# Layer 0 attention: later exponentials and totals in the short rows, and the quotient written over its own PSUM bank

## The chip, the cores and the metric

One core of one Trainium2 chip. The metric is the device time of one execution in microseconds (us). Times inside the execution come from one profiled run; "ns" is used for single instructions. The engines are called PE (matmul), PEld (its weight load), DVE (vector), ACT (scalar), POOL (GpSimd) and SP (it issues the DMAs).

## The reference, cut to what matters

Two layers are added to an input x of shape 1 x 128 x 256 x 256. The change touches layer 0 alone:

```
# layer 0; x is group-normalised first; 128 rows s, 256 positions r, 8 heads of 32 channels
bias   = einsum('nijz,zh->nhij', pair_repr, bias_proj)
gate   = sigmoid(msa @ gate_proj)
q,k,v  = split(msa @ qkv_proj)
sim    = softmax(einsum('nsqhc,nskhc->nshqk', q, k) / sqrt(32)) + bias
attend = einsum('nshqk,nskhc->nsqhc', sim, v) * gate
x      = x + attend @ out_proj
```

The softmax is not divided before the product with v. With E the exponentials of the scores, a row is computed as (E v) / (sum of E) + (bias v), then gated. Layer 1 is a banded attention of 4 heads with 64 channels; its code is not changed.

## The kernel before, in words

**Rows and pairs.** The loop at line 1092 runs over the 128 rows s. Projections are made for two rows at once, in a form with seven products instead of eight (class `Seven`, lines 592 to 634). A pair of rows has one *even* row, in whose second half the projections q and k of a later pair are made ("qk", order EARLY), and one *odd* row with v and the gate ("vg", order PLAIN) and the output projection of an older pair. The even row is the short one.

**Order within a row s.** On PE: scores of heads 0 to 3 (`sim`, line 837), row sums of the row before (`zs`, line 882), in odd rows one product of bias and values (`pbv`, line 933), E v of the row before (`av`, line 869), scores of heads 4 to 7, then the *stretch*, a list of projection products of about 0.43 us each (line 590) with bias products among them. PE, ACT, DVE and SP follow the program's order exactly, since the block at line 1078 is scheduled by hand; POOL is not in that list.

**The stretch.** `two_of_them` (line 639) reads the order string word by word. `fA` and `gA` are the first two products of the two projections f and g, followed by an ACT copy of the whole bank (line 622). `f3`, `f6`, `f7`, `f4`, `f2` are single products; after 6 and 7 ACT copies half a bank to `mid` (lines 624, 626), after 4 a whole bank (line 628). `x` calls `rest`, `d` takes the next job from `work`, `b` the next bias product, `p` the next output product. The products accumulate in one bank, so product 3 overwrites half of the bank only after the copy at 622, product 7 only after the copy at 624, and product 4 only after the copy at 626.

**ACT's exponentials.** Each half of a row has four banks of scores; one exponential (line 850) empties one. Three are issued at once, the fourth in the first half of a row after `join_tiles`, in the second half at `x`. `totals` (line 983) follows at `x`: ACT copies the sums `zs` of the row before and also writes out the accumulated sum, which the profile shows as a second instruction at line 988.

**DVE's chain.** `divide` (line 958) takes the reciprocal of `zs` and sends it through DRAM so that it comes back spread over all partitions as `near`. `weighted` (line 1005) multiplies `av` by `near` (line 1011). `gated` runs two rows later, as the first of a row's own DVE work: it adds bias times values (line 1022) and multiplies by the gate (line 1023). `least` (line 991) takes the smallest sum.

**PSUM.** Eight banks: five in a ring shared by scores and projections, and one each for `z`, `bv` and `av`. With one bank for `av`, the `av` product of a row starts when every reader of the older one has finished; before, the last reader is the product in `weighted`, which writes to a tile `t` in SBUF.

The lines that set this up in a row are:

```python
last_exp = scores(s, 0)
gated(s - 2)
zs = sum_heads(s - 1)
divide(s - 1, zs)
...
attend(s - 1)
```

Of the kernel before, what the change touches and what calls it, by code (L numbers as in the profile page):

```python
# [9 lines left out]
F32 = mybir.dt.float32  # L10
AF = mybir.ActivationFunctionType
ALU = mybir.AluOpType
# [3 lines left out]
P = 128  # L16
R = 256
# [22 lines left out]
def conv_preact_kernel(  # L40
# [14 lines left out]
    nc = tc.nc  # L55
    S = x.shape[1]
# [69 lines left out]
    for part, first in ((seen[:, 0], 0), (seen_high, -KB)):  # L126
        nc.gpsimd.memset(part, 1.0)
        for b in range(NB):
            d = first + KB * b - QLO[b]
# [504 lines left out]
            nc.gpsimd.tensor_tensor(self.to[:, 2:4], self.to[:, 2:4], self.mid, ALU.add)  # L634

    PLAIN = "fA gA x f2 p f3 f6 p g3 g6 p f7 b p g7 f4 p b g4 p g2 b p"
    EARLY = "fA gA x d b f3 f6 g3 g6 d f7 f2 g7 f4 b d g4 g2 d b"

    def two_of_them(pool, f, g, name, order, rest, bias, po, work):

# [133 lines left out]
    with ExitStack() as both:  # L774
# [21 lines left out]
        with ExitStack() as lay0:  # L796
            row = lay0.enter_context(tc.tile_pool(name="row0", bufs=2))
            att = lay0.enter_context(tc.tile_pool(name="att0", bufs=2))
            st, hd, outs = {}, {}, {}
# [29 lines left out]
            def scores(s, half):  # L829
                i, r = divmod(s, 2)  # L830
                q, k = res["q", i], res["k", i]
                sims = [sim_bank(f"sim{s}_{half}_{j}") for j in range(4)]
                for kt in range(2):
                    for c in range(2):
                        for j in range(4):
                            p0, k0 = D0 * j, kt * P + KB * c
                            nc.tensor.matmul(  # L837
                                sims[j][KB * c : KB * (c + 1), kt, :],
                                lhsT=k[p0 : p0 + D0, 2 * r + half, k0 : k0 + KB],
                                rhs=q[p0 : p0 + D0, 2 * r + half, :],  # L840
                                start=True, stop=True,
                            )
                ex = att.tile([P, 4, 2, R], F32, tag="ex", name=f"ex{s}_{half}", bufs=3)
                both = att.tile([P, 4, R], F32, tag="both", name=f"both{s}_{half}")
                hd[s, half] = (ex, both)


                def weigh(js):
                    for j in js:
                        nc.scalar.activation(ex[:, j], sims[j], AF.Exp, scale=1.0 / math.sqrt(D0))  # L850

                weigh(range(3))
                return lambda: weigh((3,))

            def join_tiles(s, half, j):

                if s < S:
                    ex, both = hd[s, half]
                    nc.vector.tensor_tensor(both[:, j : j + 2], ex[:, j : j + 2, 0, :], ex[:, j : j + 2, 1, :], ALU.add)  # L859
# [98 lines left out]
            def divide(s, zs):  # L958
                if s < 0:
                    return  # L960
                rz = att.tile([P, R], F32, tag="rz", name=f"rz{s}", bufs=1)
                nc.vector.reciprocal(rz, zs[:, 0, :])  # L962
                near = att.tile([P, 2, R], F32, tag="near", name=f"near{s}", bufs=1)
                if s < S - 1:
                    far = rz0_far[s % 2]
                    nc.sync.dma_start(out=far.rearrange("j h q -> (j h) q"), in_=rz[0 : P : B // 2])
                    for j in range(A):
                        nc.sync.dma_start(
                            out=near[strip(j)].rearrange("p h q -> p (h q)"),
                            in_=far[j].rearrange("h q -> (h q)").partition_broadcast(B),  # L970
                        )
                hd[s, "rz"] = rz
                hd[s, "z"] = (zs, near)

            def spread_last(s):

                rz, near = hd[s, "rz"], hd[s, "z"][1]
                ps = proj_bank(f"near{s}")
                for half in range(2):
                    nc.tensor.matmul(ps[:, half, :], lhsT=spread0[:, half], rhs=rz, start=True, stop=True)  # L980
                nc.scalar.copy(near, ps)

            def totals(s):

                if s >= 0:
                    zs = hd[s, "z"][0]
                    z = att.tile([P, R], F32, tag="z", name=f"z{s}", bufs=1)
                    nc.scalar.activation(z, zs[:, 0, :], AF.Identity, accum_out=zsum[:, s : s + 1])
                    hd[s, "least"] = z

            def least(s):

                if s >= 0:
                    z = hd.pop((s, "least"))
                    nc.vector.tensor_reduce(zmin[:, s : s + 1], z, axis=AX.X, op=ALU.min)
# [9 lines left out]
            def weighted(s):  # L1005

                if s < 0:
                    return
                av, near = hd.pop((s, "av")), hd.pop((s, "z"))[1]
                t = hd[s, "t"] = att.tile([P, 2, R], F32, tag="t", name=f"t{s}", bufs=1)  # L1010
                nc.vector.tensor_tensor(t, av, near, ALU.mult)  # L1011

            def gated(s):

                if s < 0:
                    return
                i, r = divmod(s, 2)
                if r == 0:
                    ats[i] = row.tile([P, 4, R], F32, tag="at", name=f"at{i}", bufs=1)
                st[s]["at"] = at = ats[i][:, 2 * r : 2 * r + 2, :]  # L1020
                t = hd.pop((s, "t"))
                nc.vector.tensor_tensor(t, hd.pop(s), t, ALU.add)  # L1022
                nc.vector.scalar_tensor_tensor(  # L1023
                    at, res["g", i][:, 2 * r : 2 * r + 2, :], 1.0, t, op0=ALU.add, op1=ALU.mult
                )
# [52 lines left out]
            with tc.manual_schedule(  # L1078
# [11 lines left out]
                nc.sync.dma_start(out=bias_far, in_=bias_blocks[0, 1])  # L1090
                most1 = Most(st1, stats1, 3, 1)
                for s in range(S):
                    last_exp = scores(s, 0)
                    gated(s - 2)
                    zs = sum_heads(s - 1)
                    divide(s - 1, zs)
                    join_tiles(s, 0, 0)
                    last_exp()
                    if s % 2 == 1:
                        e = res["g", s // 2]  # L1100
                        nc.scalar.activation(e, e, AF.Tanh, scale=0.5)
                    if s % 2 == 0:
                        bias = biased(s // 2)
                    else:
                        next(bias)
                    attend(s - 1)
                    join_tiles(s, 0, 2)
                    if s == 0:
                        sum_bias()
                    if s % 2 == 0:  # L1110
                        settle_pair((s - 4) // 2)
                    if S - 3 <= s < S - 1:
                        most1.join(s - S + 3)
                    normal(s + 4)
                    last_exp = scores(s, 1)
                    if s == 4:
                        for weights in quarters1.values():
                            weights.sum()
                    work = (
                        lambda: join_tiles(s, 1, 0), lambda: join_tiles(s, 1, 2),  # L1120
                        lambda: weighted(s - 1), lambda: least(s - 1),
                    )

                    def rest():

                        last_exp()
                        totals(s - 1)

                    po = iter(())
                    if s % 2 == 1 and s > 1:  # L1130
                        out_sums((s - 3) // 2)
                        po, work = output((s - 3) // 2, work), ()
                    if s < S - 2:
                        stretch(
                            ("qk", "vg")[s % 2], s // 2 + 1, (EARLY, PLAIN)[s % 2], rest, bias, po,
                            work if s % 2 == 0 else (),
                        )
                        work = work if s % 2 == 1 else ()
                    else:
                        rest()  # L1140
                        for _ in range(2 if s % 2 == 0 else 3):
                            next(bias)
                            next(po, None)
                            next(po, None)
                        for _ in po:
                            pass
                        if s % 2 == 0:
                            next(bias)
                    for job in work:
                        job()  # L1150
                    if s % 2 == 1 and s < S - 2:
                        sum_rows((s + 3) // 2)
                        sum_values(s // 2 + 1)
# [7 lines left out]
                        nc.tensor.matmul(warm[:, 0, :], lhsT=ident, rhs=out_sb[:, 0, :], start=True, stop=True)  # L1161

                gated(S - 2)
                divide(S - 1, sum_heads(S - 1))
                totals(S - 1)
                attend(S - 1)
# [17 lines left out]
        with ExitStack() as lay:  # L1184
# [4 lines left out]
            att = lay.enter_context(tc.tile_pool(name="att1", bufs=2))  # L1189
# [268 lines left out]
            with tc.manual_schedule(engines={  # L1458
# [12 lines left out]
                for i in range(last):  # L1471
                    s = 2 * i
# [266 lines left out]
```

## Time and profile before

| what | value |
|---|---|
| median of 3 runs | 3120.62 us (3120.52 to 3124.83) |
| the profiled execution's own time | 3121.14 us |
| its span, first to last instruction | 3119.4 us |
| exponentials of layer 0 (line 850) | from 209.2 to 2028.0 us, 1024 of them |
| granted TensorE clock, mean | 0.992 |
| DVE, busy from 430 to 830 us | 353.85 us |
| ACT, busy from 430 to 830 us | 270.06 us |
| POOL, busy from 430 to 830 us | 272.73 us |
| L962 reciprocal, 128 of them | 1745 ns each |
| L995 smallest sum, mean | 408 ns each |

The profiled execution takes 1.7 us more than its span, which lies outside the first and the last instruction. In a timeline a line has the start in us from the span's start, the duration, the engine, the source line, the operation and the tiles (output, arrow, inputs); "idle before" is in square brackets. A matmul's end is modelled and overlaps the next one's start, so the spacing of starts tells how fast PE really goes. `x8` or `x16` are the instructions merged into the line.

### The profile page before, as it was taken

Reading aid. Unit: us, or ns where it says so; the run is one execution under the profiler, and the core shown is the slowest. Engines: PE = TensorE matmul, PEld = TensorE weight load, DVE = VectorE, ACT = ScalarE, POOL = GpSimd, SP = SyncE. Lnnn points to the kernel's source line nnn. Section 1 sums busy time; section 2 is a strip of 40 time slices with the busy share of each in tenths; the row PEclk is TensorE's granted clock in tenths of the full one; section 3 lists DMA queues with packets and bytes.
Section 4 is the critical chain, followed back from the end, with each engine's and each line's share of the span. In section 5 each row is a group of like instructions: output and inputs, shape, how many; then the busy total and the mean of one; then the engine's idle time right before and its main releaser. Section 6 shows DMA issues by size and latency. Waiting matters only on the chain.

```text
span 3119.4 us, 142735 instructions
## 1 busy us (share of the span) xinstructions
PE 3028.8 (97%) x62733; PEld 2048.6 (66%) x62733; DVE 2422.4 (78%) x4523; ACT 1904.3 (61%) x4321; POOL 2015.4 (65%) x1916
## 2 busy tenths in 40 slices
PE   6779999999999999999999999999999999999997
PEld 4546666666666666666666666567777777777775
DVE  4668888888888888898888888856666666666665
ACT  4656666666666666666666666645555555555553
POOL 3036667666766666676667666647677777777774
PEclk8989999999999999999999999999999999999999
DMA  9942222222222222222122222124444444444443
GB/s 375 424 129 55 50 65 61 57 55 65 61 50 62 65 61 49 63 65 61 48 65 62 60 51 65 41 65 98 104 99 103 99 96 104 100 101 100 96 102 71
DMA packets 384790, 280.86 MB, mean 90 GB/s; under 512 B 285232, under 2 KB 353312, under 8 KB 378016
## 3 DMA queue, kind: packets, MB, share of 16 engines
q1 hardware_dynamic: 383264, 269.29, 33.0%
q8 instruction: 494, 8.09, 1.1%
q0 software_dynamic: 752, 2.36, 0.2%
q14 instruction: 136, 1.11, 0.1%
q10 hardware_dynamic: 144, 0.00, 0.0%
HBM read 202.38 MB, written 69.18 MB: 87 GB/s over the span
## 4 chain that ended last, share of the span: by engine, by line
PE 91%; DMA 5%; DVE 2%; POOL 1%; issue 1%; ACT 0%; SPq 0%; DVEq 0%; POOLq 0%; ACTq 0%
PE sim L837 8%; PE p1v L1260 7%; PE av L869 7%; PE p1q L590 7%; PE pbv L933 6%; PE po L590 6%; PE pq L590 6%; PE p1o L590 6%; PE p1k L590 6%; PE pv L590 6%; PE pk L590 5%; PE pg L590 5%; PE zs L882 4%; PE 1sim L1281 3%; DMA pr<-in_L_conv_pair_repr_dram 3%; PE 1av L1322 3%
## 5 line engine op out<-in xcount | busy, mean ns | idle before, releaser
L850 ACT ACTIVATE ex<-sim 128x512 f32<-128x512 f32 x1024 | 549.8, 608 | 281.2 <-PE sim L837 281.2
L859 DVE TENSOR_TENSOR both<-ex 128x512 f32<-128x512 f32 x512 | 471.0, 948 | 13.4 <-ACT ex L850 13.2
L634 POOL TENSOR_TENSOR v<-v,midv 128x512 f32<-128x512 f32 x64 | 82.3, 1285 | 401.1 <-ACT v L628 401.1
L837 PE MATMUL sim<-q,k 32*64 32x256 f32 x8192 | 289.8, 389 | 1.3 <-ACT ex L850 1.3
L869 PE MATMUL av<-ex,v 128*32 128x256 f32 x4096 | 244.5, 379 | 0.0
L1291 POOL TENSOR_TENSOR 1p<-1ex,seen 128x768 f32<-128x768 f32 x127 | 231.5, 1823 | 12.5 <-ACT 1ex L1289 12.5
L694 ACT ACTIVATE 1q<-p1q,bqk 128x256 f32<-128x256 f32 x192 | 90.9, 473 | 240.2 <-PE p1q L590 121.8
L1260 PE MATMUL p1v<-w_in_t,1xn 128*64 128x128 f32 x4096 | 236.3, 273 | 0.1
L1260 PEld LDWEIGHTS p1v<-w_in_t,1xn 128*64 128x64 f32 x4096 | 231.5, 137 | 6.0 <-issue 0.5
L962 DVE RECIPROCAL rz<-zs 128x256 f32<-128x256 f32 x128 | 223.3, 1745 | 6.1 <-PE zs L882 6.1
L582 POOL TENSOR_TENSOR 1ts<-1xn 128x512 f32<-128x512 f32 x64 | 81.3, 1271 | 226.8 <-ACT 1xn L1221 226.8
L837 PEld LDWEIGHTS sim<-q,k 32*64 32x64 f32 x8192 | 152.4, 131 | 113.5 <-issue 41.9
L1023 DVE SCALAR_TENSOR_TENSOR at<-g,t 128x512 f32<-128x512 f32 x128 | 202.6, 1583 | 9.2 <-DVE t L1022 0.5
L1391 DVE TENSOR_TENSOR 1at<-1av,1near 128x512 f32<-128x512 f32 x128 | 82.5, 686 | 137.2 <-DMA 1near<-rz_far 108.3
L634 POOL TENSOR_TENSOR q<-q,midq 128x512 f32<-128x512 f32 x64 | 82.2, 1285 | 157.9 <-ACT q L628 157.9
L869 PEld LDWEIGHTS av<-ex,v 128*32 128x32 f32 x4096 | 131.8, 110 | 77.1 <-DVE t L1011 0.5
L1298 POOL TENSOR_TENSOR 1zp<-1p 128x512 f32<-128x512 f32 x127 | 162.4, 1278 | 10.0
L1267 ACT COPY 1v<-p1v 128x512 f32<-128x512 f32 x128 | 75.0, 586 | 125.0 <-PE p1v L1260 125.0
L346 DVE BATCH_NORM_STATS2 stats<-xs 128x6 f32<-128x128 f32 x512 | 100.3, 277 | 64.7 <-DMA xs<-in_x_dram 64.7
L723 DVE TENSOR_TENSOR o<-po,xt 128x256 f32<-128x256 f32 x189 | 80.2, 424 | 77.8 <-PE po L590 72.0
L882 PE MATMUL zs<-both,place 128*32 128x256 f32 x2048 | 138.8, 388 | 0.5 <-DVE both L859 0.5
L688 DVE SCALAR_TENSOR_TENSOR 1o<-p1o,bo_v,yg 128x256 f32<-128x256 f32 x183 | 88.5, 483 | 56.0 <-PE p1o L590 53.2
(340 smaller groups left out, 8564.4 us busy)
## 6 DMA issues: line engine op xcount, KB each, us to landing
pr<-in_L_conv_pair_repr_dram SPq DMA_DIRECT2D x32, 1024.0 KB
xs<-in_x_dram SPq DMA_DIRECT2D x16, 2048.0 KB
x<-o SPq DMA_DIRECT2D x64, 512.0 KB
yg<-x SPq DMA_DIRECT2D x64, 512.0 KB
out_dram<-1o SPq DMA_DIRECT2D x256, 128.0 KB
near<-rz_far SPq DMA_DIRECT2D x508, 64.0 KB
xg<-in_x_dram SPq DMA_DIRECT2D x252, 128.0 KB
1near<-rz_far SPq DMA_DIRECT2D x124, 256.0 KB
```

Source lines behind the costliest of these rows:

```text
L590: nc.tensor.matmul(out[cols], lhsT=lhsT[:, cols], rhs=rhs, **flags)
L634: nc.gpsimd.tensor_tensor(self.to[:, 2:4], self.to[:, 2:4], self.mid, ALU.add)
L837: nc.tensor.matmul(sims[j][KB * c : KB * (c + 1), kt, :], lhsT=k[p0 : p0 + D0, 2 * r + half, k0 : k0 + KB], rhs=q[p0 : p0 + D0, 2 * r + ha ...
L850: nc.scalar.activation(ex[:, j], sims[j], AF.Exp, scale=1.0 / math.sqrt(D0))
L859: nc.vector.tensor_tensor(both[:, j : j + 2], ex[:, j : j + 2, 0, :], ex[:, j : j + 2, 1, :], ALU.add)
L869: nc.tensor.matmul(to[D0 * j : D0 * (j + 1), half, :], lhsT=v[:, 2 * r + half, c0 : c0 + D0], rhs=weights(4 * half + j, kt), start=(kt == ...
L882: nc.tensor.matmul(zs[strip(j), 0, :], lhsT=place0[:, half, :], rhs=both[:, j, :], start=(half == 0), stop=(half == 1),)
L933: nc.tensor.matmul(ps[strip(j), acc, half, :], lhsT=stationary[n][:, half, strip(j)], rhs=bias_of[n][:, 4 * half + j, :], start=(n <= 2 an ...
L962: nc.vector.reciprocal(rz, zs[:, 0, :])
L1023: nc.vector.scalar_tensor_tensor(at, res["g", i][:, 2 * r : 2 * r + 2, :], 1.0, t, op0=ALU.add, op1=ALU.mult)
L1260: nc.tensor.matmul(ps[KB * half : KB * (half + 1), b, :], lhsT=xns[i][:, 2 * r + kt, KB * b : KB * (b + 1)], rhs=w_in_t[:, kt, 2 * C + P * ...
L1291: engine.tensor_tensor(p.rearrange("p j (r c) -> p (j r) c", c=WROW)[:, :, 0 : 2 * WSTEP] .rearrange("p r (t c) -> p r t c", c=WSTEP)[:, : ...
```

## The change

Five things are edited, all in layer 0.

1. The exponentials. `scores` now issues two at once and returns the other two. In the first half of a row both follow after `join_tiles`. In the second half of odd rows (and of the last two rows) the third is issued at once and the fourth at `x`, as before. In the second half of even rows the order string has two `x`: the third comes between the copy of `fA` and the copy of `gA`, the fourth after the copy of `g6`.
2. `totals` moves from `x` to the end of the stretch, after its last copies.
3. `least` leaves the list of jobs and runs one row later, after the second `join_tiles`; for row S - 2 it runs after the loop.
4. In EARLY the bias product after `gA` comes ahead of the first job, and the later jobs are moved by a few places. The order of the PE products is the same.
5. The quotient (product of `av` and `near`) is written over `av` in its PSUM bank, the addition of `gated` works in place there, and the tile `t` is gone.

```diff
-    EARLY = "fA gA x d b f3 f6 g3 g6 d f7 f2 g7 f4 b d g4 g2 d b"
+    EARLY = "fA x gA b d f3 f6 g3 g6 x f7 f2 g7 f4 d b g4 d g2 b"
...
-                weigh(range(3))
-                return lambda: weigh((3,))
+                weigh(range(2))
+                return (lambda: weigh((2,))), (lambda: weigh((3,)))
...
-                av, near = hd.pop((s, "av")), hd.pop((s, "z"))[1]
-                t = hd[s, "t"] = att.tile([P, 2, R], F32, tag="t", name=f"t{s}", bufs=1)
-                nc.vector.tensor_tensor(t, av, near, ALU.mult)
+                av, near = hd.pop((s, "av")), hd.pop((s, "near"))
+                nc.vector.tensor_tensor(av, av, near, ALU.mult)
+                hd[s, "t"] = av
...
-                nc.vector.tensor_tensor(t, hd.pop(s), t, ALU.add)
+                nc.vector.tensor_tensor(t, t, hd.pop(s), ALU.add)
...
-                    last_exp = scores(s, 0)
+                    exps = scores(s, 0)
                     gated(s - 2)
                     zs = sum_heads(s - 1)
                     divide(s - 1, zs)
                     join_tiles(s, 0, 0)
-                    last_exp()
+                    for exp in exps:
+                        exp()
...
                     attend(s - 1)
                     join_tiles(s, 0, 2)
+                    least(s - 2)
...
-                    last_exp = scores(s, 1)
+                    third, fourth = scores(s, 1)
+                    if s % 2 == 1 or s >= S - 2:
+                        third()
...
                     work = (
                         lambda: join_tiles(s, 1, 0), lambda: join_tiles(s, 1, 2),
-                        lambda: weighted(s - 1), lambda: least(s - 1),
+                        lambda: weighted(s - 1),
                     )
 
+                    rests = iter((third, fourth) if s % 2 == 0 and s < S - 2 else (fourth,))
+
                     def rest():
 
-                        last_exp()
-                        totals(s - 1)
+                        next(rests)()
...
+                    totals(s - 1)
                     for job in work:
                         job()
...
                 gated(S - 2)
+                least(S - 2)
                 divide(S - 1, sum_heads(S - 1))
                 totals(S - 1)
```

More of the change, by code (lines that the diff above doesn't have):

```diff
@@ L972, in divide @@
                 hd[s, "rz"] = rz
-                hd[s, "z"] = (zs, near)
+                hd[s, "zs"], hd[s, "near"] = zs, near
             def spread_last(s):
-                rz, near = hd[s, "rz"], hd[s, "z"][1]
+                rz, near = hd[s, "rz"], hd[s, "near"]
                 ps = proj_bank(f"near{s}")
@@ L985, in totals @@
                 if s >= 0:
-                    zs = hd[s, "z"][0]
+                    zs = hd.pop((s, "zs"))
                     z = att.tile([P, R], F32, tag="z", name=f"z{s}", bufs=1)
```

## The prediction, made before the changed kernel ran

> **What bounds the kernel now.** I read the page's busy times and its chain of work first, then busy time by window, then the timeline of one pair of rows engine by engine, and last the single lines of DVE.
>
> ```profile
> PE 3028.8 (97%) x62733; PEld 2048.6 (66%) x62733; DVE 2422.4 (78%) x4523; ACT 1904.3 (61%) x4321; POOL 2015.4 (65%) x1916
> PE 91%; DMA 5%; DVE 2%; POOL 1%; issue 1%; ACT 0%; SPq 0%; DVEq 0%; POOLq 0%; ACTq 0%
> ```
>
> PE carries the chain. In the middle of layer 0 the windows show it busy without a break, at full clock:
>
> ```profile
> 430.00:830.00 400.00, 400.00 (x9455) 253.95 (x9450) 353.85 (x534) 270.06 (x604) 272.73 (x254) 1.00 0.25 59
> ```
>
> That busy share hides small waits, since matmuls overlap. They show in the spacing of starts. An even row begins at 1011.52 and the next at 1040.00, so a pair takes 28.47 us, the same from pair to pair. A projection product takes 0.43 us from start to start; in the even row some starts come later:
>
> ```profile
> 1013.46 1.91 PE L869 MATMUL av<-ex,v 128*32 128x256 f32 x32
> 1018.10 0.62 PE L933 MATMUL pbv<-bias_sb,v 128*32 128x128 f32 x16
> 1018.64 0.64 PE L590 MATMUL pq<-xn,sums_q 128*32 128x256 f32 x8
> 1019.10 0.61 PE L590 MATMUL pq<-ts,sums_q 128*32 128x256 f32 x8
> ...
> 1019.96 0.61 PE L590 MATMUL pk<-ts,sums_k 128*32 128x256 f32 x8
> 1020.54 0.64 PE L590 MATMUL pq<-ts,sums_q 128*32 128x256 f32 x8
> 1021.00 0.61 PE L590 MATMUL p2qk<-xn,qkv_sb 128*32 128x256 f32 x8
> ```
>
> The step to 1018.64 (product f3) is 0.54 and the one after it 0.46; the step to 1020.54 (f7) is 0.58 and the next 0.46. Against 0.433 this is 0.107 + 0.027 + 0.147 + 0.027 = **0.31 us in each pair**. The list of waits names ACT for both, and ACT's timeline says why:
>
> ```profile
> PEld pq L590 <- ACT midq L624: 27.3, 63, 0.4
> PEld pq L590 <- ACT q L622: 11.9, 62, 0.2
> ```
>
> ```profile
> 1017.98 0.61 ACT L622 COPY q<-pq 128x512 f32<-128x512 f32 x1
> ...
> 1018.92 0.66 ACT L850 ACTIVATE ex<-sim 128x512 f32<-128x512 f32 x1
> 1019.41 0.45 ACT L988 ACTIVATE z<-zs 128x256 f32<-128x256 f32 x1
> 1019.68 0.26 ACT L988 ACTIVATION_READ_ACCUMULATOR z<-zs 128x1 f32 x1
> 1019.77 0.43 ACT L943 COPY bv<-pbv 128x256 f32<-128x256 f32 x1
> 1020.12 0.37 ACT L624 COPY midq<-pq 128x256 f32<-128x256 f32 x1
> 1020.70 0.37 ACT L624 COPY midk<-pk 128x256 f32<-128x256 f32 x1 [0.21 <-PE pk L590]
> ```
>
> The copy of fA ends at 1018.59 behind three exponentials, and f3 starts 0.05 later. The copy after f6 ends at 1020.49 behind the fourth exponential and the totals, and f7 starts 0.05 later. The odd row shows no such step. DVE is late nowhere for PE, but slow in the gate's two instructions:
>
> ```profile
> 1011.66 0.42 DVE L723 TENSOR_TENSOR o<-po,xt 128x256 f32<-128x256 f32 x1 [0.88 <-PE po L590]
> 1012.00 1.17 DVE L1022 TENSOR_TENSOR t<-bv,t 128x512 f32<-128x512 f32 x1
> 1013.28 1.58 DVE L1023 SCALAR_TENSOR_TENSOR at<-g,t 128x512 f32<-128x512 f32 x1
> ```
>
> ```profile
> L1011 DVE TENSOR_TENSOR t<-av,near x128: 676/680/692, 243.6 to 2040.2; 128x512 f32<-128x512 f32 x128
> L1022 DVE TENSOR_TENSOR t<-bv,t x128: 679/792/1522, 244.6 to 2040.9; 128x512 f32<-128x512 f32 x128
> L1023 DVE SCALAR_TENSOR_TENSOR at<-g,t x128: 691/1592/1658, 246.2 to 2041.6; 128x512 f32<-128x512 f32 x128
> ```
>
> [...] L1022 and L1023, both inputs in SBUF, spread from 0.68 to 1.5 and 1.66 us; L1011, with `av` in PSUM, never leaves 676 to 692 ns, also at 1023.39, where POOL's sum over q is running. [...]
>
> **The change, part by part.**
>
> *Gain, f3 and f7.* The exponentials of this half start at 1016.54 and follow each other by 0.49, so with two of them ahead the copy of fA starts at 1017.52 (its second product ends at 1016.80 + 0.61) and ends at 1018.13, ahead of f3's due time 1018.10 + 0.43. The totals leave, so the copy after f6 follows f6 freely and f7 doesn't wait. That removes 0.31.
>
> *New wait, f4.* The fourth exponential now stands between the copy after g6 and the copy after f7, and f4 overwrites what the latter reads. From the start of g6: the copy starts 0.74 later (1019.96 to 1020.70); a 256-column instruction gives way after 0.27 (1019.41 to 1019.68), so the exponential starts at 1.01; the next starts 0.49 after it (1018.92 to 1019.41), at 1.50; the copy after f7 takes 0.37 and PE 0.05 more, 1.92. f4 is due four products after g6, at 1.73. That is 0.19, and 0.027 for the longer step behind a wait: **0.215**. ACT has 0.21 + 0.17 of idle time around this point, but in pieces too short for a 0.49 exponential.
>
> *New wait, av of the even row.* Its bank is now held by `gated`. The first two times are fixed by the last output product of the odd row: L723 at 1011.66, L1022 at 1012.00. With one input in PSUM, L1022 takes 0.68 (L1011's value), so it ends at 1012.68; L1023 follows after the 0.11 seen now (1013.17 to 1013.28) at 1012.79, takes 0.69, ends at 1013.48; PE can start at 1013.53, against 1013.46 now: 0.07, with the longer step **0.10**. In the odd row `av` comes 0.43 later behind a bias product, and `gated` starts at the row's beginning without the output sum ahead of it: over half a us to spare. What queues behind a late `av` on PE is everything, starting with the second half's scores. The write into PSUM is shown by no row. From below it is 0.68. [...] I take 0.68.
>
> *Totals at the end.* The next row's `zs` product overwrites the bank that totals reads, and now waits for it. In the even row the last ACT copy (L947) starts 0.76 after the last bias product; 0.27, 0.27 and 0.26 more to the end of the accumulator's read make 1.56, and PE could start at 1.61. `zs` is due 0.57 + 1.05 = 1.62 after that product (1023.62, 1024.19, 1025.24). So it just fits: I take **0.01**, bounds 0 and 0.10. In the odd row the totals end 0.4 us ahead of `zs`. The next exponentials wait for the scores, longer than totals take.
>
> *DVE's moves.* Its order has one job fewer in the stretch and `least` earlier. The gate's two instructions give back about 1.4 us in an even row (1.17 + 1.58 to 0.68 + 0.69) and 1.0 in an odd one. The second join waits for the fourth exponential (g6 at 8.3 us into the row, 1.01 to its start, 0.6 for itself: 9.9) and is done near 10.7, ahead of the bias sum L945, which now starts at 1023.05, 11.5 into the row, and gates the last bias product now as before. So this is worth nothing: PE hides it, and PE's waits are for ACT. Were the cover gone (L945 late by 0.1), PE would lose that 0.1. No DMA moves; the four `near` loads stand where they were behind the reciprocal, which in the even row comes up to 1 us earlier. First-half exponentials keep their order on ACT: 0. After the loop `least` stands ahead of the last reciprocal, at most 0.4 us, and the last two rows, where PE does wait for DVE, get back about as much: 0, bounds -1 and +1.
>
> *Sum.* A pair: -0.31 + 0.215 + 0.10 + 0.01 = +0.015 us; 63 pairs, +1 us. The profiled execution took 3121.14, of which 3119.4 is span, and the median of the runs is 0.5 lower. So 3121.14 + 1 = **3122 us**, no change that can be told: what moves from f3 and f7 is paid again at f4 and at av. A measurement of this kernel tells about 0.2%, 6.2 us or 0.10 us a pair.
>
> **The rivals.**
>
> *Slower: DVE in PSUM is dearer than L1011*. Place: L1022 of the even row, ahead of av. Price: each 0.1 us more costs 62 x 0.1 = 6 us; it decides from 0.09 on. With 0.2 more: 3134. [...] For it: no row writes PSUM from DVE, and av has no slack left. Against: L1011's constant 680 ns from PSUM. If the gate stayed contended in spite of the PSUM input (1.58), av would be 0.9 late and the time 3177; L1011's overlap with POOL speaks against it.
>
> *Slower by totals*: the read ends 0.1 later than worked out and `zs` waits, 63 x 0.1: 3128. For it: 0.01 us of slack. Against: it is hidden in odd rows.
>
> *Faster: a new wait doesn't come.* If f4 isn't held, because ACT gets the exponential done in its idle pieces: 63 x (-0.31 + 0.11) = -12.6, 3109. If av isn't held, 63 x -0.085 = -5, 3116. Neither: 3102. For it: two ACT gaps near f4, and a DVE that is freer by 2.4 us a pair. Against: the order of ACT is fixed, and f4's due time is known within 0.03.
>
> *It doesn't do what it says*: the f3 and f7 waits stay, since another instruction takes ACT's place ahead of the copies; 63 x 0.31 = 20 us on top, 3141. ACT has nothing else there: 1 in 20.
>
> **How the numbers follow.** As worked out, 0.42, 3117 to 3127; faster 0.20; dearer PSUM 0.23; totals 0.10; waits stay 0.05. The dearest PSUM cases and the fastest are left out, the rest gives 3107 to 3142. Faster by over 0.2%: 0.20. Within: 0.42. Slower: 0.23 + 0.10 + 0.05 = 0.38.
>
> **What would show it.** Right: even rows with 0.43 steps at f3 and f7, a step of about 0.65 at f4, `av` 2.02 to 2.04 after the even row's start instead of 1.94, L1022 and L1023 at a constant 680 to 700 ns, the pair still near 28.49 us. Wrong: f4 in step, L1022 well over 0.7 us, a late `zs` ahead of av, or a wait in the odd row, which I have left without any.

## The result and the profile after

The changed kernel takes 3124.32 us (median of 14 runs, 3122.81 to 3127.58), the kernel before 3121.34 (14 runs, 3118.66 to 3124.83). The ratio is 1.0009, 95% interval 1.0001 to 1.0017: a loss of 0.01 to 0.17%, within the 0.2% to which, by the prediction, a measurement of this kernel tells. The profiled execution has a span of 3122.6 us at a mean clock of 0.991.

The page's first row and the window that was read before, of the changed kernel (busy us and instruction counts in the order PE, PEld, DVE, ACT, POOL, then clock and DMA):

```profile
PE 3030.2 (97%) x62733; PEld 2047.4 (66%) x62733; DVE 2258.6 (72%) x4523; ACT 1907.0 (61%) x4321; POOL 1904.1 (61%) x1916
```

```profile
430.00:830.00 400.00, 399.66 (x9444) 253.49 (x9440) 317.13 (x533) 271.48 (x605) 247.76 (x254) 1.00 0.25 59
```

PE is as full as before, while DVE dropped from 353.85 to 317.13 us and POOL from 272.73 to 247.76 in the same 400 us. So a large relief of two engines did not shorten the whole. What PE waits for is seen in the starts of one even row, which begins at 1012.79 (timeline of PE):

```profile
1014.81 1.93 PE L869 MATMUL av<-ex,v 128*32 128x256 f32 x32
...
1019.47 0.62 PE L933 MATMUL pbv<-bias_sb,v 128*32 128x128 f32 x16
1019.91 0.61 PE L590 MATMUL pq<-xn,sums_q 128*32 128x256 f32 x8
1020.34 0.61 PE L590 MATMUL pq<-ts,sums_q 128*32 128x256 f32 x8
...
1021.20 0.61 PE L590 MATMUL pk<-ts,sums_k 128*32 128x256 f32 x8
1021.64 0.61 PE L590 MATMUL pq<-ts,sums_q 128*32 128x256 f32 x8
1022.07 0.61 PE L590 MATMUL p2qk<-xn,qkv_sb 128*32 128x256 f32 x8
1022.50 0.61 PE L590 MATMUL pk<-ts,sums_k 128*32 128x256 f32 x8
1023.13 0.64 PE L590 MATMUL pq<-ts,qkv_sb 128*32 128x256 f32 x8
1023.59 0.62 PE L933 MATMUL pbv<-bias_sb,v 128*32 128x128 f32 x16
```

f3 (1019.91) and f7 (1021.64) now follow in steps of 0.44 and 0.43. f4 (1023.13) comes 0.63 after g7, and the next product 0.46 later. `av` starts 2.02 us into the row; in the kernel before it started at 1.94. ACT's timeline of the same row has the reason for f4:

```profile
1018.88 0.59 ACT L622 COPY q<-pq 128x512 f32<-128x512 f32 x1
1019.35 0.63 ACT L850 ACTIVATE ex<-sim 128x512 f32<-128x512 f32 x1
...
1021.08 0.37 ACT L624 COPY midq<-pq 128x256 f32<-128x256 f32 x1 [0.35 <-PE pq L590]
1021.94 0.37 ACT L624 COPY midk<-pk 128x256 f32<-128x256 f32 x1 [0.49 <-PE pk L590]
1022.21 0.60 ACT L850 ACTIVATE ex<-sim 128x512 f32<-128x512 f32 x1
1022.70 0.38 ACT L626 COPY midq<-pq 128x256 f32<-128x256 f32 x1
```

The copy after f6 (1021.08) is free and waits for PE. The fourth exponential (1022.21) holds the copy after f7 to 1022.70; that copy ends at 1023.08, and f4 starts 0.05 later. DVE has the reason for `av`; here are its timeline at the start of the row and the lines by instruction, with those who waited for L1023:

```profile
1012.93 0.42 DVE L723 TENSOR_TENSOR o<-po,xt 128x256 f32<-128x256 f32 x1 [0.88 <-PE po L590]
1013.27 0.69 DVE L1022 TENSOR_TENSOR av<-av,bv 128x512 f32<-128x512 f32 x1
1014.06 0.69 DVE L1023 SCALAR_TENSOR_TENSOR at<-g,av 128x512 f32<-128x512 f32 x1
```

```profile
L1010 DVE TENSOR_TENSOR av<-av,near x128: 685/690/700, 243.5 to 2040.7; 128x512 f32<-128x512 f32 x128
L1022 DVE TENSOR_TENSOR av<-av,bv x128: 687/699/700, 244.3 to 2041.5; 128x512 f32<-128x512 f32 x128
L1023 DVE SCALAR_TENSOR_TENSOR at<-g,av x128: 686/687/690, 245.1 to 2042.2; 128x512 f32<-128x512 f32 x128
  PEld av L869: 25.8, 63
```

The addition and the gate take 0.69 to 0.70 us in all 128 rows. The gate ends at 1014.75, and PE, which without the wait would start `av` at 1014.73 (1.94 after the row's start), starts it at 1014.81. The 25.8 us are idle time of the weight load, which in the kernel before started 0.21 us ahead of its product (1013.25 and 1013.46) and here starts with it; about 0.10 us a pair reaches the products.

The pair of rows takes 28.454 us (median of the distances between even rows) against 28.474, so the steady part of layer 0 became 0.02 us a pair *shorter*.

### The profile page after: what moved, and what is told of

The parts are those of the page before. It is cut to its first block, busy times and chain, and to the rows that moved or that the text cites. A ratio compares the mean times of both kernels' runs of the same rounds, so it can differ in the third digit from the quotient of the medians.

```text
span 3122.6 us, 142547 instructions
## 1 busy us (share of the span) xinstructions
PE 3030.2 (97%) x62733; PEld 2047.4 (66%) x62733; DVE 2258.6 (72%) x4523; ACT 1907.0 (61%) x4321; POOL 1904.1 (61%) x1916
## 4 chain that ended last, share of the span: by engine, by line
PE 92%; DMA 4%; DVE 2%; POOL 1%; ACT 1%; issue 0%; SPq 0%; DVEq 0%; ACTq 0%; POOLq 0%
PE sim L837 9%; PE av L869 7%; PE p1v L1267 7%; PE p1q L590 7%; PE po L590 6%; PE pbv L933 6%; PE p1k L590 6%; PE p1o L590 6%; PE pq L590 6%; PE pv L590 6%; PE pg L590 5%; PE pk L590 5%; PE zs L882 4%; PE 1sim L1288 3%; DMA pr<-in_L_conv_pair_repr_dram 3%; PE 1av L1329 3%
## 5 line engine op out<-in xcount | busy, mean ns | idle before, releaser
L859 DVE TENSOR_TENSOR both<-ex 128x512 f32<-128x512 f32 x512 | 449.7, 898 | 51.0 <-ACT ex L850 50.9
L634 POOL TENSOR_TENSOR v<-v,midv 128x512 f32<-128x512 f32 x64 | 82.2, 1285 | 453.9 <-ACT v L628 453.9
L634 POOL TENSOR_TENSOR q<-q,midq 128x512 f32<-128x512 f32 x64 | 82.0, 1282 | 217.2 <-ACT q L628 217.2
L869 PEld LDWEIGHTS av<-ex,v 128*32 128x32 f32 x4096 | 125.4, 110 | 93.4 <-DVE at L1023 25.8
L723 DVE TENSOR_TENSOR o<-po,xt 128x256 f32<-128x256 f32 x189 | 80.3, 425 | 109.6 <-PE po L590 109.6
L1366 DVE RECIPROCAL 1rz<-1z 128x64 f32<-128x64 f32 (+1 forms) x192 | 129.8, 678 | 2.2
```

Of the source, the lines that this page charges most:

```text
L869: nc.tensor.matmul(to[D0 * j : D0 * (j + 1), half, :], lhsT=v[:, 2 * r + half, c0 : c0 + D0], rhs=weights(4 * half + j, kt), start=(kt == ...
```

## The experiments

The times are medians, each taken beside the kernel before on the same chip; "pair" is the median distance of even rows in the profile, "second scores" the step from an even row's first scores to its second, "odd stretch" from an odd row's second scores to the next row. Layer 0 is counted from its first scores product to layer 1's first values product.

| kernel | median us | ratio to before (95%) | pair | second scores | odd stretch | layer 0 |
|---|---|---|---|---|---|---|
| before | 3121.34 | | 28.474 | 3.777 | 11.597 | 1843.8 |
| changed | 3124.32 | 1.0009 (1.0001 to 1.0017) | 28.454 | 3.880 | 11.597 | 1844.6 |
| PSUM quotient alone | 3129.47 | 1.0020 (1.0011 to 1.0029) | 28.577 | 3.880 | 11.597 | 1851.5 |
| SBUF quotient | 3121.56 | 0.9996 (0.9987 to 1.0004) | 28.433 | 3.777 | 11.680 | 1843.7 |
| later exponential | 3108.69 | 0.9954 (0.9941 to 0.9968) | 28.230 | 3.880 | 11.596 | 1830.3 |
| SBUF and later exponential | 3108.67 | 0.9954 (0.9940 to 0.9968) | 28.200 | 3.777 | 11.670 | 1829.1 |
| SBUF, least back | 3116.64 | 0.9979 (0.9970 to 0.9987) | 28.351 | 3.777 | 11.597 | 1837.1 |
| all three | 3104.98 | 0.9944 (0.9930 to 0.9957) | 28.127 | 3.777 | 11.597 | 1825.7 |
| gate first | 3101.80 | 0.9935 (0.9921 to 0.9949) | 28.127 | 3.777 | 11.597 | 1822.3 |
| later exponential, totals back | 3115.24 | 0.9972 (0.9961 to 0.9983) | 28.325 | 3.880 | 11.597 | 1836.7 |

These are three sets of runs: the kernel before took 3123.14 us beside "PSUM quotient alone" to "SBUF and later exponential" and 3123.83 us beside the last four. Where a us matters between sets, the ratios are to be compared. Pair, steps and layer 0 come from one profile of each kernel.

**Quotient in SBUF again.** In the changed kernel:

```diff
-                nc.vector.tensor_tensor(av, av, near, ALU.mult)
-                hd[s, "t"] = av
+                t = hd[s, "t"] = att.tile([P, 2, R], F32, tag="t", name=f"t{s}", bufs=1)
+                nc.vector.tensor_tensor(t, av, near, ALU.mult)
...
-                nc.vector.tensor_tensor(t, t, hd.pop(s), ALU.add)
+                nc.vector.tensor_tensor(t, hd.pop(s), t, ALU.add)
```

> The changed kernel with the quotient in an SBUF tile again; all other edits stay. Theory 1 (f3 and f7 are freed, f4 and av pay it back, piece by piece): the step before the even row's second scores goes from 3.88 back to 3.78 us, the pair from 28.45 to 28.35, and the late av of row 2 (1.5 us, once) goes too: 8 us under the changed kernel, 3116 to 3117 where before is 3121. Theory 2 (the waits seen in the spacing are made up elsewhere, the time is set by something else, such as where the tiles lie): within 2 us of the changed kernel's 3124. If the placement of SBUF tiles is what lengthened layer 1 by 2.6 us in the changed kernel's profile, layer 1 comes back to 1068.6 from 1071.1 here.

It took 3121.56 us, by the ratios 4 us under the changed kernel where theory 1 had 8. The second scores came back to 3.777, as theory 1 has it, but the pair fell by 0.021 only: the odd row's stretch grew from 11.597 to 11.680. PE's and DVE's timelines of that stretch in this kernel:

```profile
917.20 0.61 PE L590 MATMUL po<-at,out_sb 128*32 128x256 f32 x8
...
918.07 0.62 PE L590 MATMUL pv<-sums_v,ts 128*32 128x128 f32 x16
918.57 0.64 PE L590 MATMUL po<-at,out_sb 128*32 128x256 f32 x8
```

```profile
916.48 0.41 DVE L995 TENSOR_REDUCE zmin<-z 128x1 f32<-128x256 f32 x1
...
918.10 0.41 DVE L723 TENSOR_TENSOR o<-po,xt 128x256 f32<-128x256 f32 x1
```

and DVE's and PE's in the changed kernel:

```profile
917.44 0.41 DVE L995 TENSOR_REDUCE zmin<-z 128x1 f32<-128x256 f32 x1
...
919.76 0.42 DVE L723 TENSOR_TENSOR o<-po,xt 128x256 f32<-128x256 f32 x1 [0.61 <-PE po L590]
```

```profile
919.08 0.61 PE L590 MATMUL po<-at,out_sb 128*32 128x256 f32 x8
...
920.38 0.61 PE L590 MATMUL po<-at,out_sb 128*32 128x256 f32 x8
```

With SBUF inputs the addition and the gate are long again (up to 1.67 and 1.66 us in the later kernel "SBUF, least back"), and DVE gets to the output sum L723 with no idle time: it starts 0.90 us after its product (917.20), in the changed kernel 0.68 after it (919.08), having waited 0.61 us for it. (An expectation below puts both about 0.2 too high.) The next output product, at 918.57, goes to the other half of the bank that this sum reads. It starts 0.06 after the sum's end and 0.50 after the product before it, the following one 0.45 later; in the changed kernel it starts 0.20 after the sum's end, in step. So the changed kernel needs DVE's relief in the odd row for 0.083 us a pair and pays 0.103 for it at `av`. The end of the layer loses too: from row 126 to layer 1 it takes 43.6 us against 41.9 in the changed kernel, which takes back the 1.5 us won at row 2; the cause was not looked for. Layer 1 took 1068.7 us here, as in the kernel before, but 1070.9 in the later kernel "SBUF, least back": so the quotient's place alone doesn't set it.

**Fourth exponential one place later.** In the changed kernel:

```diff
-    EARLY = "fA x gA b d f3 f6 g3 g6 x f7 f2 g7 f4 d b g4 d g2 b"
+    EARLY = "fA x gA b d f3 f6 g3 g6 f7 x f2 g7 f4 d b g4 d g2 b"
```

> The changed kernel with the fourth exponential of the even row one place later, after the copy that follows f7. Theory 1: f4's step goes from 0.63 to 0.43 and the next from 0.46 to 0.43, the pair from 28.45 to 28.23, 14 us under the changed kernel, about 3110; av stays late by 0.10. Theory 2: within 2 us of 3124.

3108.69 us and a pair of 28.230, both close to what was worked out: 0.224 us a pair was f4's wait. It is 0.46% under the kernel before.

**Both edits together.**

> Both of these edits on the changed kernel. Theory 1: no wait for ACT or DVE is left in the even row, the pair is 28.13, and the time is the sum of both, 21 to 22 us under the changed kernel, about 3102. Theory 2: as the changed kernel. If the two waits hide each other, it is no better than the better one alone, about 3110.

3108.67, over six us worse than expected, and no better than the later exponential alone. The two waits don't hide each other: the second scores are at 3.777 and f4 is in step. The odd stretch is long again (11.670), and so is the end from row 126 on (43.8 us), so this is the loss of the first experiment once more, and the number that matched "hide each other" did so for another reason.

**PSUM quotient alone, in the kernel before.** The three changed lines of edit 5 and nothing else.

> The kernel before with nothing but the quotient written over av in PSUM. Theory 1: f3 and f7 stay late, av gets late by 0.10, the pair goes from 28.47 to 28.58, and row 2 loses 1.5 us once: 7 to 8 us over before, about 3129. Should DVE's relief (its addition and gate short of 0.70 instead of 0.8 to 1.7 us) be worth something to PE: at or under before's 3121.

3129.47 and 28.577: 0.103 a pair at `av`, all of it a loss, since the kernel before had no wait for DVE in the odd row to be relieved of. Row 2's late `av` is there too (a wait of 1.70 us, once), as in the profile of the changed kernel, which is shown here. DVE comes late to the gate at this place: it waits for products with the bias until 239.85, and its two joins then take 3.39 us (3.40 in the kernel before).

```profile
240.19 3.39 DVE L859 TENSOR_TENSOR both<-ex 128x512 f32<-128x512 f32 x2
...
245.10 0.69 DVE L1023 SCALAR_TENSOR_TENSOR at<-g,av 128x512 f32<-128x512 f32 x1
245.85 1.93 PE L869 MATMUL av<-ex,v 128*32 128x256 f32 x32 [1.58 <-DVE at L1023]
```

In the kernel before, where `av` waits only for the quotient, this product starts at 244.37.

**SBUF, and the smallest sum back in the stretch.** On the kernel with the SBUF quotient:

```diff
                     join_tiles(s, 0, 2)
-                    least(s - 2)
...
-                        lambda: weighted(s - 1),
+                        lambda: weighted(s - 1), lambda: least(s - 2),
...
-    EARLY = "fA x gA b d f3 f6 g3 g6 x f7 f2 g7 f4 d b g4 d g2 b"
+    EARLY = "fA x gA b d f3 f6 g3 g6 x f7 f2 g7 f4 d b g4 d g2 d b"
```

> The changed kernel with the quotient in SBUF and the smallest sum back among the jobs of the stretch. The run with SBUF alone lost in the odd row's stretch (11.60 to 11.68) what it won at av; theory A: that is because the smallest sum stands ahead of the output sum on DVE, whose start goes from 0.88 to 1.09 us after its product. Then here the odd row is back at 11.60 with av at 3.78, the pair 28.35, 6 us under the SBUF run beside it in state, near 3117. Theory B: the lateness comes from the POOL contention of the addition and the gate alone; then the odd row stays at 11.67 and the time does too.

Theory A: the odd stretch is 11.597 again, the pair 28.351, 3116.64 us, although the addition and the gate are still slow (up to 1.67 and 1.66 us). So the lateness takes both, `least` ahead of the output sum and a slow addition and gate. The slow gate alone was there in the kernel before and cost nothing; the changed kernel has `least` alone, and that costs nothing either.

**All three.** SBUF quotient, later exponential, smallest sum back.

> SBUF quotient, later fourth exponential, smallest sum back among the jobs. Theory A: no wait for ACT or DVE above the kernel before's unavoidable steps is left; the pair is 28.12, 5 us under the run with the first two edits (3108.7 there), about 3103. Theory B: 28.20 and 3108 to 3109.

The pair is 28.127, as expected. The time is 3104.98, 3.7 us under the run without the last edit (by the ratios, which compare across the sets, about 3), where 5 were expected.

**The gate ahead of the last output sum.** On the kernel with the later exponential, with the quotient left in PSUM:

```diff
-                self.take(n)
+                if n == 4:
+                    held.append(lambda: self.take(4))
+                else:
+                    self.take(n)
...
                     gated(s - 2)
+                    take_held()
```

> The changed kernel with the later fourth exponential, the quotient still in PSUM, and the last output sum of the odd row taken after the gate of the next row instead of ahead of it. Theory 1 (av waits for the addition and the gate, which stand behind the output sum on DVE): the addition starts 0.3 instead of 0.48 us into the even row, the gate ends 0.2 earlier, av is back at 1.94, the step at 3.78, the pair 28.13, 6 us under the run with the later exponential alone (3108.7), about 3102.5. If what delays av is not DVE's order but a bank in PSUM that DVE wrote: av stays at 2.02 and the time at 3108 to 3109.

DVE's and PE's timelines of an even row (the row starts at 917.79; lines 1022 and 1023 are 1032 and 1033 here, 869 is 879 and 723 is 730):

```profile
918.03 0.70 DVE L1032 TENSOR_TENSOR av<-av,bv 128x512 f32<-128x512 f32 x1 [0.97 <-ACT bv L965]
918.83 0.69 DVE L1033 SCALAR_TENSOR_TENSOR at<-g,av 128x512 f32<-128x512 f32 x1
919.44 0.42 DVE L730 TENSOR_TENSOR o<-po,xt 128x256 f32<-128x256 f32 x1
```

```profile
917.79 1.12 PE L847 MATMUL sim<-q,k 32*64 32x256 f32 x32
...
919.73 1.91 PE L879 MATMUL av<-ex,v 128*32 128x256 f32 x32
...
927.39 0.61 PE L590 MATMUL pk<-ts,sums_k 128*32 128x256 f32 x8
927.83 0.61 PE L590 MATMUL pq<-ts,qkv_sb 128*32 128x256 f32 x8
```

The addition starts 0.24 into the row instead of 0.48, the gate ends at 919.52, and `av` is back at 1.94 with its quotient in PSUM. So `av` was late because of where the gate stood in DVE's order, not because DVE writes into the bank. f4 is in step (0.44). This run has the lowest median, 3101.80 us, 0.65% under the kernel before. Its interval overlaps that of "all three", which has the same pair, so which of the two is faster is not settled; in the profiles this one takes 40.9 us from row 126 to layer 1 and "all three" 43.3.

**Totals back behind the fourth exponential.** On the kernel with the later exponential:

```diff
-                        next(rests)()
+                        job = next(rests)
+                        job()
+                        if job is fourth:
+                            totals(s - 1)
...
-                    totals(s - 1)
                     for job in work:
```

> The changed kernel with the later fourth exponential, and the totals back behind the fourth exponential in place of the end of the stretch. Theory 1: in the even row ACT's copy after g7 starts at about 10.65 instead of 10.39, its product g4 waits 0.06 to 0.09, 4 to 6 us over the run with the later exponential alone, 3112 to 3115; the odd row is unchanged. If the totals at the end of the stretch cost something at the zs product, it is no slower than 3108.7.

3115.24 against 3108.69 (ratios 0.9972 and 0.9954), pair +0.095. ACT's and PE's timelines:

```profile
933.67 0.60 ACT L850 ACTIVATE ex<-sim 128x512 f32<-128x512 f32 x1
934.16 0.39 ACT L988 ACTIVATE z<-zs 128x256 f32<-128x256 f32 x1
934.42 0.21 ACT L988 ACTIVATION_READ_ACCUMULATOR z<-zs 128x1 f32 x1
934.52 0.39 ACT L626 COPY midk<-pk 128x256 f32<-128x256 f32 x1
```

```profile
934.45 0.62 PE L933 MATMUL pbv<-bias_sb,v 128*32 128x128 f32 x16
934.95 0.64 PE L590 MATMUL pk<-ts,qkv_sb 128*32 128x256 f32 x8
```

The copy after g7 ends at 934.91 and g4 starts at 934.95, a step of 0.50 followed by 0.46. So moving the totals to the end is worth 0.095 us a pair with this order, and costs nothing at `zs`, which comes 1.05 after its scores either way.

## Why the prediction was right, point by point

Forecast: 3122 us, no change that can be told. Measured: 3124.32, 1.0009 of before. The steps:

- *f3 and f7 freed, 0.31 a pair*: both steps are 0.43 to 0.44 in the changed kernel. The gain is 0.29 by the medians of the steps, since a step after a bias product is 0.437 even without a wait. Held; no run puts the old order of the exponentials back alone.
- *f4's new wait, 0.215*: 0.63 and 0.46 against 0.433 make 0.224, and taking it away shortened the pair by 0.224. Held, and shown by the later exponential.
- *`av`'s new wait, 0.10*: 0.103, shown by the PSUM quotient alone and by the gate put first. The addition takes 0.70 where 0.68 was taken, so the rival of a dear PSUM falls; how dear it could have been, 0.2 more in the prediction, was the author's estimate.
- *Totals at the end, 0.01*: 0. From scores to `zs` it is 1.05 us as before.
- *DVE's moves worth nothing*: right as a sum, wrong as worked out, so this term came out by luck. Moving `least` ahead of the output sum would cost PE 0.083 us a pair in the odd row; DVE's relief through PSUM hides it. The prediction gave that relief no worth, left the odd row without any wait, and looked only at what `least` would gain or lose in the even row and after the loop.
- *Left out*: the start. Row 2's `av` waits once for the gate of row 0, which DVE reaches late there, 1.5 us. And a gain: the bias sum L945, which the last bias product of the even row waits for (its weight load starts 0.12 us after L945's end in both kernels), starts 0.68 us after its product (1023.59 to 1024.27) where it took 0.76 (1022.29 to 1023.05), and the last two steps of the even row shrink from 0.46 and 0.57 to 0.43 and 0.55, 0.05 a pair. In the trace L945 had a separate semaphore wait in all 64 pairs before and has one left now. The likely reason is that the second join, ahead of it on DVE, waits for the fourth exponential (0.56 us, to 1022.85), which now comes behind the ACT copy (L943) that L945 also needs (1020.30, the exponential at 1022.21; in the kernel before 1019.77 and 1018.92); this is the author's estimate, and no run tests it alone.

The pair was to grow by 0.015 and shrank by 0.020. As measured it is -0.293 + 0.224 + 0.103 + 0 - 0.053 = -0.019: the gain that was left out makes the difference, and the small errors of the other terms nearly cancel. Over 63 pairs this is -1.3 us, and with row 2 and a few single late steps layer 0 is 0.9 us longer than before in the profiles. So the mechanism of each large term was right, but that the whole comes so close to the forecast is in part luck: the gain left out, about 3 us over the layer, is offset by row 2 and by layer 1. The rest of the 3 us lies in layer 1, 1071.2 us against 1068.6, whose code is the same. In the ten profiles of this study it took 1068.6 to 1071.4 us, so a single profile can't assign it; whether the small excess of the median is more than the start's 1.5 us stays open.

## What to carry to other kernels

When an instruction is moved out of the way of one product, lay the engine's whole queue against the next due times: here the fourth exponential was moved from one copy PE waits for to just ahead of another, and one place later it was free. Here the PSUM bank written in place was held until its last reader, the gate (it ended at 1014.75, `av` started at 1014.81), so what mattered was where the gate stood in its engine's order; putting it ahead of an unhurried sum kept the quotient in the bank and lost the wait. And two edits that look free can be paying for each other, as the quotient in PSUM did here for the moved `least`, which only undoing one alone shows.

## What the runs showed of the hardware

- DVE in place on a PSUM bank (128x512 fp32, one input in SBUF) took 0.69 to 0.70 us in the median, against 0.68 for PSUM to SBUF in the kernel before: 0.02 us more at most.
- The addition and the gate with both inputs in SBUF took up to 1.52 and 1.66 us in the kernel before, with one in PSUM never over 0.70. In 125 of the 128 rows POOL was at work throughout both; there they took 0.70 to 1.52 and 1.03 to 1.66 us with SBUF inputs, and 0.69 to 0.70 and 0.69 in the changed kernel. In the three rows without POOL (additions at 2020.87, 2035.21 and 2040.92 in the kernel before) they took 0.68 to 0.69 and 0.69 with SBUF inputs. So it was beside POOL's work that they were slow. POOL gained as well, 25 us in 400 (its L634 on k, beside the gate, took 1.74 us at 1024.44 in the kernel before and 1.29 at 1025.73 in the changed one), and lost it again with the quotient in SBUF (273.20 in the same window).
- A PE step that waited cost its lateness and 0.02 to 0.03 us in the step after it (0.456 in place of 0.432 after f4 and g4, 1.864 in place of 1.840 after `av`); at f4, `av`, g4 and the late output product of the SBUF quotient, PE started 0.04 to 0.06 us after the end of what it waited for. It wasn't so everywhere: behind L945 the last bias product of the kernel before started 0.15 us after the sum's end.
